# The output projection's low-weight products behind a flag read on the chip, and reordered seams, in a three-part decoder layer

## The chip, the cores and the metric

The kernel runs on one core of one Trainium2 chip. The metric is the device time of one execution in microseconds (us). Five engines work at once and wait for each other through semaphores: TensorE (PE, with its weight loads shown apart as PEld), VectorE (DVE), ScalarE (ACT), GpSimd (POOL) and SyncE (SP), which here issues all DMAs. Products are written to PSUM, in eight banks of 128 x 512 float32; the kernel uses four under the name `ps` and four under the name `pa`. POOL doesn't read PSUM here.

## The reference

One layer on 8 sequences of 112 tokens, 512 wide, in three parts, each added to x:

```
x = x + self_attention(layernorm(x))            # 16 heads of 32, rotary, causal, plain float32
x = x + cross_block(layernorm(x), ctx_2048)     # below
x = x + ffn(layernorm(x))                       # ternary weights, silu(gate) * up, rms norm

# cross_block
ln_out = LN(h)
q, k, v, qx = fp8_linear(ln_out, wq/wk/wv/wqx)              # inputs rounded to fp8
core = attention of q (16 heads of 128) on k, v (8 heads)   # over the 112 own tokens
kx, vx = split(ctx @ w_kv_x)                                # 375 context tokens, float32
xout = attention of qx on kx, vx
catq = fp8_round(concat(core, xout) / proj_smooth)
return (catq @ wproj.T) * (proj_in_scale * proj_w_scale)    # 4096 -> 512
```

The weight `wproj` is made by `_fp8_roundtrip(w / sc)`: a float32 array whose values are fp8 numbers. `w_kv_x` is a plain float32 array.

## The kernel before, in words

**Numbers.** Where a product must be as exact as float32, the kernel splits a float32 operand into a high part `hi` (rounded to float32r, the format of PE's faster products) and a low part `lo = w - hi`, and issues two products into one bank. `split_chunk(s, what, k)` (L288) does that for one 128 x 512 chunk of weights of strip `s`: `what` 0 is q, 1 is k and v, 2 is the output projection. For `what` 2 it copies on ACT and subtracts on POOL (L300, L301), then frees the raw tile, which starts the next raw load on SP (`load_raw`, L268).

**Work units.** The cross block is 8 strips of heads, 4 of the own attention and 4 of the context attention, by 8 batches: 64 units, `Own` (0 to 31) and `Context` (32 to 63). A unit's `project` is its spine on PE; between its pieces it calls `advance(stage, g)`, which runs a named stage (`normed`, `turn`, `score`, `weigh`, `turn_p`, `attend`, `rounded`, `out`) of earlier units, each with a lag in units written in `stages`. So the order on each engine is written out by hand; there is no scheduler. Rows of 7 token tiles of 128 don't match 8 batches of 112, so a unit with b of 1 to 7 also finishes tile b - 1: `rounded` (L752) rounds that tile to `cq` on ACT, DVE and POOL, and `project_out` (L704) multiplies `cq` with the strip's weights: for each of four 128-row pieces a `hi` and a `lo` product through `both` (L688, products at L691), eight into one bank, and then DVE adds the scaled bank to `xs` (L713). In the last strip DVE also takes the tile's norm statistics there (`stats3`).

**The stages in time.** Self-attention (L373 to L679) runs in plain float32: `project_qk` makes q and k for four batches at a time (PE, ACT's bias L433, DVE's shuffle, POOL's two rotary passes L444 and L446), then `batch` interleaves values, scores, softmax (DVE, POOL, ACT's exp L511), turns of p (ACT's copies L524) and their products. `transposed` (L408) turns the normed input by PE and ACT's copies L418. Then come the own units, then the context units, in whose keys the products of L912 stand, twelve for each of three pieces. During the context units the feed-forward weights are made ternary (L1119 to L1164).

**The drain and the feed-forward part.** Behind the last unit, a loop over n from 1 to 3 runs the open stages in the order of one tuple, and a table `between` puts pieces of the feed-forward part after some of them: `ffn_input(0)` (norm, L161, turns by PE, L1227, ACT's copy L1229 and DVE's subtraction L1230 for tiles 0 to 3) after the last scores, and four `hidden_part`s (sixteen products each at L1256, ACT's silu L1264) after later stages. Then `ffn_input(1)` takes tiles 4 to 6. The feed-forward part runs eight hidden steps and four `down` steps (L1389). In the last `down`, the root mean square is found (one-column products at L1405, L1409, POOL's power L133), and DVE finishes each tile with two passes (L1414, L1415), after which SP stores it (L1416).

Of the kernel before, what the change touches and what calls it, by code (L numbers as in the profile page):

```python
# [11 lines left out]
F32 = mybir.dt.float32  # L12
F32R = mybir.dt.float32r
BF = mybir.dt.bfloat16
U16 = mybir.dt.uint16
AF = mybir.ActivationFunctionType
ALU = mybir.AluOpType
AX = mybir.AxisListType

P = 128  # L20
# [3 lines left out]
KC = H // P  # L24
NT = B * S // P
# [14 lines left out]
def decoder_layer(  # L40
# [10 lines left out]
    wdown: bass.AP,  # L51
    out: bass.AP,
):

# [5 lines left out]
    nc = tc.nc  # L62
# [12 lines left out]
    def uid(s):  # L75
        count[0] += 1
        return f"{s}_{count[0]}"

    def ps():
        return psum.tile([P, 512], F32, tag="ps", name=uid("ps"))  # L80
# [5 lines left out]
    def sm(what, n, bufs=None):  # L86
        return small.tile([P, n], F32, tag=f"{what}{n}", name=uid(what), bufs=bufs)
# [7 lines left out]
    xb, xs = [], []  # L95
# [19 lines left out]
    nc.gpsimd.memset(gones, 0.0)  # L115
    nc.gpsimd.memset(gones[0:64, 0:64], 1.0 / 128.0)
    nc.gpsimd.memset(gones[64:128, 64:128], 1.0 / 128.0)


    idle = ps()  # L120
# [9 lines left out]
    def power(dst):  # L130

        rows, n = dst.shape
        nc.gpsimd.tensor_tensor(dst, dst, expo[:rows, :n], ALU.pow)  # L133
# [80 lines left out]
    raws, split = {}, {}  # L214
# [73 lines left out]
    def split_chunk(s, what, k):  # L288

        w = raws.pop((s, what, k))  # L290
        if what == 1 and s > 3:
            hi, mix, lo = [ring.tile("CBA", "wx") for _ in range(3)]
            nc.scalar.copy(hi, w)  # L293
            nc.gpsimd.tensor_tensor(w, w, hi.bitcast(F32), ALU.subtract)
            split[s, what, k] = hi, mix, lo
            opened.append((w, hi, mix, lo))
            return
        hi, lo = [ring.tile(("ABC", "B", "AB")[what], i) for i in ("hi", "lo")]
        if what == 2:
            nc.scalar.copy(hi, w)  # L300
            nc.gpsimd.tensor_tensor(lo, w, hi.bitcast(F32), ALU.subtract)  # L301
        else:
            if what == 0:
                cuts = [(slice(0, 512), 0 if s < 4 else 3)]
            else:
                cuts = [(slice(0, 256), 1), (slice(256, 512), 2)]
            for cut, m in cuts:
                c = col(V_INS + 4 * m + k)
                nc.scalar.activation(hi[:, cut], w[:, cut], AF.Copy, scale=c)
                nc.vector.scalar_tensor_tensor(  # L310
                    lo[:, cut], w[:, cut], c, hi[:, cut].bitcast(F32), ALU.mult, ALU.subtract
                )
        split[s, what, k] = hi, lo
        load_raw()
# [58 lines left out]
    with ExitStack() as st:  # L373
# [22 lines left out]
        w_v = load_qkv(wqkv[2], a1, 4)  # L396
        vb = a1.tile([S, H], F32, tag="vb", name="vb")
        nc.sync.dma_start(out=vb, in_=vbias.partition_broadcast(S))

        hT = a1.tile([P, KC, B * S], F32, tag="hT", name="hT")  # L400
        lns, hs = {}, {}
# [193 lines left out]

        for i, oc in enumerate((0, 4, 1, 5, 2, 6, 3, 7)):
            project_qk(0, oc)
            if i == 1:
                for b in range(HB, B):
                    lns[b] = norm_stats(xb[b])  # L600
            elif i == 2:
                for b in range(HB, B):
                    ln_apply(b)
            elif i == 3:
                transposed(1)
# [17 lines left out]
        def batch(b, last, begin=0):  # L623


            least = last - HB
            if b < last:
                va[b] = values(b)
            if b - 2 >= least:
                attended(b - 2, va.pop(b - 2), pt.pop(b - 2))  # L630
            if b < last:
                banks = scores(b)
            if least <= b - 1 < last:
                pt[b - 1] = turned(pr.pop(b - 1))
            for _ in range(begin):
                quantise_begin()
            if b < last:
                pr[b] = softmaxed(banks, b >= HB)

        for b in range(HB):  # L640
            batch(b, HB)
        for i, oc in enumerate((0, 4, 1, 5, 2, 6, 3, 7)):
            project_qk(1, oc)
            if i < 2:
                batch(HB + i, HB)
            if i < HB + 2:
                joined(i, 0, HB)
            if i == HB + 2:
                for _ in range(4):
                    quantise_begin()  # L650
            elif i == HB + 3:
                quantise(4, False)
# [32 lines left out]
    for k in range(KC):  # L685
        split_chunk(0, 1, k)

    def both(out_, lhsT, parts, cut, first, last):  # L688

        for i, part in enumerate(parts):  # L690
            nc.tensor.matmul(  # L691
                out_, lhsT=lhsT, rhs=part[:, cut], start=first and i == 0, stop=last and i == 1
            )
# [10 lines left out]
    def project_out(u):  # L704

        if u.b == 0:
            return
        t, po = u.b - 1, ps()
        for j in range(4):
            both(po, u.cq[:, j * P : (j + 1) * P], split[u.s, 2, j], slice(0, 512), j == 0, j == 3)  # L710
        if u.b == NT:
            drop(u.s, 2)
        nc.vector.scalar_tensor_tensor(xs[t], po, psc, xs[t], ALU.mult, ALU.add)  # L713
        if u.s == 7:
            stats3[t] = norm_stats(xs[t])
# [497 lines left out]
                nc.gpsimd.tensor_scalar_mul(d[k], ts[k // 2][:, k % 2, :], 2.0)  # L1213
        wfs[what, i] = d

    def ffn_input(half):
        cols = CUTS[half]
        n, hs = cols.stop - cols.start, []
        for i in range(n // P):
            t = cols.start // P + i  # L1220
            h = f0.tile([P, H], F32, tag="sg", name=uid("h"), bufs=4)
            norm_apply(h, xs[t], *stats3[t])
            hs.append(h)
        for k in range(KC):
            tp = ps()
            for i, h in enumerate(hs):
                nc.tensor.transpose(tp[:, i * P : (i + 1) * P], h[:, k * P : (k + 1) * P], ident)  # L1227
            hi, lo = [ring.tile("AB", "h3T", n) for _ in range(2)]
            nc.scalar.copy(hi, tp[:, :n])  # L1229
            nc.vector.tensor_tensor(lo, tp[:, :n], hi.bitcast(F32), ALU.subtract)  # L1230
            hT[half, k] = hi, lo
# [124 lines left out]
    def hidden(u, pool):  # L1356
# [3 lines left out]

    hidden(0, f0)

    between = {
        (1, "score"): lambda: ffn_input(0),
        (2, "out"): lambda: hidden_part(0, 0, 0),
        (2, "turn_p"): lambda: hidden_part(0, 1, 0),
        (2, "rounded"): lambda: hidden_part(1, 0, 0),
        (3, "out"): lambda: hidden_part(1, 1, 0),
    }
    for n in range(1, 4):  # L1370
        live = [v for v in live if v.at < len(v.stages)]
        for stage in ("normed", "weigh", "out", "turn_p", "attend", "turn", "rounded", "score"):
            advance(stage, len(units) - 1 + n)
            if (n, stage) in between:
                between[n, stage]()

    attention.close()
    f1 = ctx.enter_context(tc.tile_pool(name="f1", bufs=1))
    tpool.append(ctx.enter_context(tc.tile_pool(name="tern2", bufs=1)))
    ffn_input(1)  # L1380
    expand_w("down", 0)
    ys = [f1.tile([P, H], F32, tag=f"y{t}", name=f"y{t}") for t in range(NT)]
    def down(c, hid, last):
        wd, pos = wfs.pop(("down", c)), []
        for t in range(NT):
            po = ps()
            for k in range(4):
                for part_ in range(2):
                    nc.tensor.matmul(  # L1389
                        po,  # L1390
                        lhsT=hid[part_][:, k, t * P : (t + 1) * P],
                        rhs=wd[k],
                        start=(k == 0 and part_ == 0),
                        stop=(k == 3 and part_ == 1),
                    )
            if c == 0:
                nc.vector.tensor_copy(ys[t], po)
            elif not last:
                nc.vector.tensor_tensor(ys[t], ys[t], po, ALU.add)
            else:  # L1400
                pos.append(po)
            if last and t == 1:
                pr = ps()
                for i in range(NT):
                    nc.tensor.matmul(  # L1405
                        pr[:, i : i + 1], lhsT=sq[:, i * P : (i + 1) * P], rhs=ones1, start=True, stop=True
                    )
                rstd = sm("rms", NT)
                nc.vector.tensor_scalar(rstd, pr[:, 0:NT], 1.0 / FF, RMS_EPS, ALU.mult, ALU.add)  # L1409
                power(rstd)  # L1410
            while last and t > 0 and pos:
                i = t + 1 - len(pos)
                r = rstd[:, i : i + 1]
                nc.vector.scalar_tensor_tensor(ys[i], ys[i], r, xs[i], ALU.mult, ALU.add)  # L1414
                nc.vector.scalar_tensor_tensor(ys[i], pos.pop(0), r, ys[i], ALU.mult, ALU.add)  # L1415
                nc.sync.dma_start(out=out[i * P : (i + 1) * P, :], in_=ys[i])  # L1416

        ring.free(*wd)
# [119 lines left out]
```

## Time and profile before

| | us |
|---|---|
| median of 3 runs | 1285.17 (1284.61 to 1287.16) |
| the profiled execution | 1283.86 |
| its span, first to last instruction | 1282.1 |
| PE busy in the span | 1200.6 |
| DVE, ACT, POOL busy | 931.8, 815.8, 846.1 |
| the `lo` products of the output projection, records in all | 88.4 (224 of 395 ns) |
| POOL's subtractions L301 | 41.9 (32 of 1316 ns) |

How to read the lines that follow: a group's line gives engine, operation, out<-in by the program's names, shapes, the count after an x, and times. A timeline line gives the start and the duration in us, and in brackets how long the engine was idle just before and whose result ended that. A table by stretches gives, for each engine, the busy time and the number of instructions, then the mean granted TensorE clock, the DMA engines' share and GB/s. The slices cut the span into 40 equal parts and give the busy share of each in tenths. Records of products overlap: the rate is read from start to start.

### The profile page before, as it was taken

The page shows a single profiled execution, that of the slowest core. Times are in us where ns is not written, and L with a number is a line of the kernel's source. Part 1 is how long each engine was busy: PE and PEld are TensorE (multiplying, and loading weights), DVE is VectorE, ACT ScalarE, POOL GpSimd, SP SyncE. Part 2 cuts the span into 40 slices and gives each one's busy share as a digit, 9 for nine tenths or more (in the row PEclk, how much of TensorE's full clock was granted, in tenths as well). Part 3 has the DMA queues.
Part 4 walks back from the last instruction along what each step waited for, and adds up shares of the span by engine and source line. Part 5 has one row for each costly group of instructions (what it writes and reads, how often), then busy time and mean ns, then how long its engine had stood idle before and what let it go on. Part 6 is the DMA issues. An engine that isn't in the chain of part 4 may idle for free. (4 is left out here: it accounts for less than half of the span.)

```text
span 1282.1 us, 19634 instructions
## 1 busy us (share of the span) xinstructions
PE 1200.6 (94%) x6326; PEld 962.4 (75%) x6326; DVE 931.8 (73%) x2366; ACT 815.8 (64%) x2008; POOL 846.1 (66%) x938
## 2 busy tenths in 40 slices
PE   8997976889999889999999999999999998899998
PEld 5673765777888767888788778788777786687876
DVE  6647986887888866677776776677777775579864
ACT  2334676878687757667667767777667665456432
POOL 6657866687877756765767656667566655477762
PEclk9988886999999999999999999999999999999999
DMA  5001120213332354455554455554544440133201
GB/s 172 1 1 42 34 91 17 83 50 106 131 127 93 122 209 152 147 201 194 182 174 151 151 171 174 162 170 161 174 150 148 167 157 5 34 107 104 73 29 58
DMA packets 55511, 149.85 MB, mean 117 GB/s; under 512 B 6400, under 2 KB 15744, under 8 KB 55408
## 3 DMA queue, kind: packets, MB, share of 16 engines
q1 hardware_dynamic: 55408, 148.59, 35.3%
q8 instruction: 50, 0.82, 0.3%
q14 instruction: 53, 0.43, 0.1%
HBM read 120.18 MB, written 26.56 MB: 114 GB/s over the span
## 5 line engine op out<-in xcount | busy, mean ns | idle before, releaser
L912 PE MATMUL pa<-wx,ct 128*125 128x512 f32 x1152 | 289.4, 400 | 2.4 <-ACT wx L293 1.5
L912 PEld LDWEIGHTS pa<-wx,ct 128*125 128x125 f32 x1152 | 208.9, 186 | 51.2 <-ACT wx L293 1.9
L210 POOL TENSOR_TENSOR f8t<-y,big 128x512 f32<-128x512 bf16 (+1 forms) x88 | 107.4, 1224 | 140.2 <-DVE big L208 139.8
L738 POOL TENSOR_TENSOR p<-p,ri 112x448 f32<-112x448 f32 (+1 forms) x64 | 118.1, 1846 | 35.6 <-DVE ri L736 35.4
L923 DVE TENSOR_TENSOR kv<-kv,pa 125x512 f32<-125x512 f32 x96 | 65.9, 687 | 98.7 <-PE pa L912 52.2
L691 PE MATMUL pa<-hi,xq 128*128 128x512 f32 (+2 forms) x352 | 112.9, 345 | 11.0 <-DVE xq L368 9.2
L997 ACT ACTIVATE p<-ps,cmx 112x375 f32<-112x375 f32 x128 | 71.8, 574 | 75.5 <-DVE cmx L996 75.5
L1256 PE MATMUL pa<-h3T,wf 128*128 128x512 f32 (+1 forms) x512 | 110.0, 371 | 2.7 <-DVE sg L1266 2.7
L691 PE MATMUL pa<-lo,xq 128*128 128x512 f32 (+2 forms) x352 | 107.5, 331 | 0.9 <-DVE lo L310 0.9
L1256 PEld LDWEIGHTS pa<-h3T,wf 128*128 128x128 f32 x512 | 92.9, 188 | 14.9 <-DVE sg L1266 3.6
L174 DVE BATCH_NORM_AGGREGATE mv<-bst 128x2 f32<-128x6 f32 (+1 forms) x472 | 86.0, 182 | 16.3
L691 PE MATMUL ps<-hi,cq 128*128 128x512 f32 x224 | 90.8, 405 | 2.8 <-POOL cq L758 1.1
L730 ACT ACTIVATE qT<-ps,hln 128x448 f32<-128x448 f32 (+6 forms) x112 | 57.4, 567 | 56.1 <-PE ps L725 55.8
L691 PE MATMUL ps<-lo,cq 128*128 128x512 f32 x224 | 88.4, 395 | 0.0
L173 DVE BATCH_NORM_STATS2 bst<-pa 128x6 f32<-128x128 f32 x280 | 76.2, 272 | 16.2 <-PE pa L691 16.2
L988 PE MATMUL ps<-kT,qT 128*112 128x375 f32 x256 | 86.0, 478 | 0.5 <-ACT kT L974 0.5
L1158 POOL TENSOR_TENSOR th<-th,tw 128x512 bf16<-128x512 bf16 x48 | 59.1, 1231 | 40.1 <-DVE th L1150 40.1
L193 ACT ACTIVATE kv<-kv,ckvnm,ckvr 125x128 f32<-125x128 f32 x192 | 77.5, 491 | 6.2 <-POOL ckvnm L189 5.5
L691 PEld LDWEIGHTS pa<-hi,xq 128*128 128x128 f32 (+1 forms) x352 | 67.9, 193 | 17.3 <-DVE xq L368 10.7
L1021 PE MATMUL ps<-pT,kv 125*128 125x224 f32 x384 | 78.0, 353 | 0.0
L1021 PEld LDWEIGHTS ps<-pT,kv 125*128 125x128 f32 x384 | 72.6, 190 | 2.0
L691 PEld LDWEIGHTS pa<-lo,xq 128*128 128x128 f32 (+1 forms) x352 | 68.0, 193 | 7.4 <-DVE lo L310 3.8
(181 smaller groups left out, 3131.1 us busy)
## 6 DMA issues: line engine op xcount, KB each, us to landing
ct<-forms SPq DMA_DIRECT2D x84, 750.0 KB, 4.4
w<-in_wattn SPq DMA_DIRECT2D x96, 256.0 KB, 3.1
forms<-form SPq DMA_DIRECT2D x12, 750.0 KB, 4.7
forms<-ct SPq DMA_DIRECT2D x12, 750.0 KB, 5.1
tr<-in_wgu SPq DMA_DIRECT2D x32, 256.0 KB, 4.5
done<-th SPq DMA_DIRECT2D x48, 128.0 KB, 4.3
wh<-done SPq DMA_DIRECT2D x24, 256.0 KB, 3.7
tr<-in_wdown SPq DMA_DIRECT2D x16, 256.0 KB, 4.4
```

Source lines behind the costliest of these rows:

```text
L173: nc.vector.bn_stats(st[: self.rows], a)
L174: nc.vector.bn_aggr(self.mv[: self.rows, self.at, :], st[: self.rows])
L193: nc.scalar.activation(dst, src, AF.Identity, bias=self.nm[:rows, i : i + 1], scale=self.r[:rows, i : i + 1])
L210: nc.gpsimd.tensor_tensor(t, y16, big, ALU.add)
L691: nc.tensor.matmul(out_, lhsT=lhsT, rhs=part[:, cut], start=first and i == 0, stop=last and i == 1)
L738: nc.gpsimd.tensor_tensor(u.p, u.p, bc, ALU.mult)
L912: nc.tensor.matmul(banks[bank][:CJ, :], lhsT=ct[:, at : at + CJ] if ct.dtype == F32R else ct[:, at : at + CJ].bitcast(F32R), rhs=split[sel ...
L923: nc.vector.tensor_tensor(kv, kv, banks[1][:CJ, :], ALU.add)
L988: nc.tensor.matmul(pp[:S, :SC], lhsT=qT[:, j, :], rhs=self.kT[:, j // 2, :], start=True, stop=True,)
L997: nc.scalar.activation(self.p[:, j, :], pp[:S, :SC], AF.Exp, bias=nm[:S], accum_out=self.sums[:S, j : j + 1])
L1021: nc.tensor.matmul(po[:, cut], lhsT=self.kv[j][:, 256 + g * P : 256 + (g + 1) * P], rhs=self.pT[:, j, cut], start=(j == 0), stop=(j == NJ ...
L1256: nc.tensor.matmul(pp[:, :n], lhsT=wcur[k][:, m * 256 + blk * P : m * 256 + (blk + 1) * P], rhs=hT[half, k][i], start=(k == 0 and i == 0), ...
```

## The change

Early on, while self-attention runs, SP loads all eight strips' output-projection weights whole (1.05 MB each, two buffers), and ACT reads the low 16 bits of every float32 as integers and sums them (`look`). DVE and one PE product add the sums up, and DVE writes 1 to `flag` if the sum is above zero, else 0. PE and POOL each read the flag into a register ahead of the first unit. From then on POOL makes the low weights, and PE issues the four low products of a projection, only if the register is above 0. If it is 0, PE issues four one-column products of zeros in their place, and POOL's semaphore is stepped without work. The conditions cut the program into blocks: all five engines jump at each of the 88.

The other edits are at the seams. `ffn_input` becomes three functions, and the table `between` a written-out order: the norms and turns of tiles 0 to 3 go ahead of the turns of p of the last unit but one, and their split ahead of the last scores; two `hidden_part`s stand right behind the last scores; tiles 4 and 5 are turned ahead of the last projection, tile 6 behind the last of those `hidden_part`s. Turns are written into `pa` banks for tiles 0 to 3, and into two `ps` and two `pa` banks for the rest. In the last `down`, ACT and POOL make the first of the two passes for tiles 3 to 6.

```diff
+    flag = const.tile([1, 1], mybir.dt.int32, tag="flag", name="flag")
+    zero = const.tile([P, 1], BF, tag="zero", name="zero")
+    nc.gpsimd.memset(zero, 0.0)
...
             nc.scalar.copy(hi, w)
-            nc.gpsimd.tensor_tensor(lo, w, hi.bitcast(F32), ALU.subtract)
+            with tc.If(low_split > 0):
+                nc.gpsimd.tensor_tensor(lo, w, hi.bitcast(F32), ALU.subtract)
...
+        seen = a1.tile([P, 16], F32, tag="seen", name="seen")
+        looked = []
+        def look_load():
+            i = len(looked)
+            if i < 8:
+                w = a0.tile([P, KC * 512], F32, tag="wp", name=uid("wp"))
+                nc.sync.dma_start(out=w.rearrange("p (k o) -> p k o", k=KC), in_=wattn[i, 2])
+                looked.append(w)
+        def look(i):
+            w = looked[i].bitcast(U16).rearrange("p (n two) -> p n two", two=2)
+            for h in range(2):
+                low = w[:, h * 1024 : (h + 1) * 1024, 0:1].rearrange("p n o -> p (n o)")
+                nc.scalar.activation(low, low, AF.Copy, accum_out=seen[:, 2 * i + h : 2 * i + h + 1])
+            look_load()
+        for _ in range(2):
+            look_load()
...
             project_qk(0, oc)
+            if i in (3, 5, 7):
+                look(i // 2 - 1)
...
             batch(b, HB)
+            look(3 + b)
...
             project_qk(1, oc)
+            if i == 0:
+                look(7)
+            elif i == 2:
+                total = sm("seen", 1)
+                nc.vector.tensor_reduce(total, seen, AX.X, ALU.add)
+                pc = ps()
+                nc.tensor.matmul(pc[:1, 0:1], lhsT=total, rhs=ones1, start=True, stop=True)
+                nc.vector.tensor_scalar(flag, pc[:1, 0:1], 0.0, None, ALU.is_gt)
...
+    low = nc.values_load(flag[0:1, 0:1], engines=[mybir.EngineType.PE], min_val=0, max_val=1)
+    low_split = nc.values_load(flag[0:1, 0:1], engines=[mybir.EngineType.Pool], min_val=0, max_val=1)
...
-        for j in range(4):
-            both(po, u.cq[:, j * P : (j + 1) * P], split[u.s, 2, j], slice(0, 512), j == 0, j == 3)
+        def product(j, i, **kw):
+            nc.tensor.matmul(po, lhsT=u.cq[:, j * P : (j + 1) * P], rhs=split[u.s, 2, j][i], **kw)
+        product(0, 0, start=True, stop=False)
+        with tc.If(low > 0) as branch:
+            for j in range(4):
+                product(j, 1, start=False, stop=False)
+        with branch.Else():
+            for j in range(4):
+                nc.tensor.matmul(po[:1, 0:1], lhsT=zero, rhs=zero, start=False, stop=False)
+        for j in range(1, 4):
+            product(j, 0, start=False, stop=j == 3)
...
+    live = [v for v in live if v.at < len(v.stages)]
+    input_norms(0, 1)
+    last(1, "normed", "weigh")
+    input_norms(2, 3)
+    last(1, "out")
+    input_turns(0, 0, 1, 2, 3)
+    last(1, "turn_p", "attend", "turn", "rounded")
+    input_splits(0)
+    last(1, "score")
+    hidden_part(0, 0, 0)
+    last(2, "weigh")
+    hidden_part(0, 1, 0)
+    last(2, "turn_p", "out", "attend")
+    input_norms(4, 5)
+    last(2, "rounded")
+    hidden_part(1, 0, 0)
+    input_turns(1, 4, 5)
+    last(3, "out")
+    input_norms(6)
+    hidden_part(1, 1, 0)
...
-    ffn_input(1)
+    input_turns(1, 6)
+    input_splits(1)
...
                 power(rstd)
+                for i in range(3, NT):
+                    nc.scalar.activation(ys[i], ys[i], AF.Copy, scale=rstd[:, i : i + 1])
+                    nc.gpsimd.tensor_tensor(ys[i], ys[i], xs[i], ALU.add)
             while last and t > 0 and pos:
...
-                nc.vector.scalar_tensor_tensor(ys[i], ys[i], r, xs[i], ALU.mult, ALU.add)
+                if i < 3:
+                    nc.vector.scalar_tensor_tensor(ys[i], ys[i], r, xs[i], ALU.mult, ALU.add)
                 nc.vector.scalar_tensor_tensor(ys[i], pos.pop(0), r, ys[i], ALU.mult, ALU.add)
```

More of the change, by code (lines that the diff above doesn't have):

```diff
@@ L1214, in expand_w, with input_norms, input_turns, input_splits @@
         wfs[what, i] = d
[L1216 to L1220, printed above, removed]
+    inputs = {}
+    def input_norms(*ts):
+        for t in ts:
             h = f0.tile([P, H], F32, tag="sg", name=uid("h"), bufs=4)
             norm_apply(h, xs[t], *stats3[t])
[L1223 to L1227, printed above, removed]
+            inputs[t] = h
+    def input_turns(half, *ts):
+        first = CUTS[half].start // P
+        if ts[0] == first:
+            inputs["banks", half] = [f() for f in ((ps, ps, pa, pa) if half else (pa,) * KC)]
+        for t in ts:
+            h = inputs.pop(t)
+            for k, tp in enumerate(inputs["banks", half]):
+                nc.tensor.transpose(
+                    tp[:, (t - first) * P : (t - first + 1) * P], h[:, k * P : (k + 1) * P], ident
+                )
+    def input_splits(half):
+        n = CUTS[half].stop - CUTS[half].start
+        for k, tp in enumerate(inputs.pop(("banks", half))):
             hi, lo = [ring.tile("AB", "h3T", n) for _ in range(2)]
@@ L1361, in decoder_layer, with last @@
     hidden(0, f0)
[L1363 to L1372, printed above, removed]
-            advance(stage, len(units) - 1 + n)
-            if (n, stage) in between:
-                between[n, stage]()
+    def last(n, *stages):
+        for stage in stages:
+            advance(stage, len(units) - 1 + n)
+    live = [v for v in live if v.at < len(v.stages)]
[18 more added lines that the diff above has]
+    hidden_part(1, 1, 0)
+    assert not any(v.at < len(v.stages) for v in live)
     attention.close()
```

## The prediction

> **What bounds the kernel now.** I read the page's busy shares and slices first, then the busy times cut at the borders of the stages (seen in the timeline: self-attention to 164 us, the ramp to 233, own units to 459, context units to 1078, the drain to 1122, the feed-forward part, the tail from 1264).
>
> ```profile
> span 1282.1 us, 19634 instructions
> PE 1200.6 (94%) x6326; PEld 962.4 (75%) x6326; DVE 931.8 (73%) x2366; ACT 815.8 (64%) x2008; POOL 846.1 (66%) x938
> ...
> PE   8997976889999889999999999999999998899998
> ...
> PEclk9988886999999999999999999999999999999999
> ```
> ```profile
> core 0: us, PE busy (x) PEld busy (x) DVE busy (x) ACT busy (x) POOL busy (x), PEclk, DMA share, GB/s
> ...
> 233.00:459.00 226.00, 205.84 (x1309) 177.72 (x1307) 188.14 (x544) 174.91 (x538) 173.35 (x215) 0.99 0.32 110
> 459.00:1078.00 619.00, 607.33 (x2934) 485.24 (x2934) 438.81 (x1211) 429.46 (x1029) 397.18 (x443) 1.00 0.49 161
> 1078.00:1122.00 44.00, 35.88 (x176) 28.19 (x177) 21.87 (x43) 20.43 (x47) 18.63 (x18) 1.00 0.08 25
> ```
> TensorE sets the time. In the context stage it is busy 607.3 of 619 us (98%) and the next engine, DVE, 71%: what leaves PE there leaves the span. In the own stage PE has 91%, but DVE 83%, ACT and POOL 77%: a cut of PE is paid out in part. In the drain PE has 82%: its waits can be had by another order.
>
> How much a low product costs is read from the starts, since records overlap (mean 395 ns). All four lines are of one output projection in the timeline:
> ```profile
> 714.88 0.39 PE L691 MATMUL ps<-hi,cq 128*128 128x512 f32 x1
> ...
> 715.10 0.39 PE L691 MATMUL ps<-lo,cq 128*128 128x512 f32 x1
> ...
> 715.33 0.39 PE L691 MATMUL ps<-hi,cq 128*128 128x512 f32 x1
> ...
> 715.56 0.39 PE L691 MATMUL ps<-lo,cq 128*128 128x512 f32 x1
> ```
> Start to start 0.227 us.
>
> **1. The low products.** 56 projections (8 strips, 7 tiles) issue four each: 224 x 0.2265 = 50.7 us off PE, if the flag is 0. It should be: the weights are values rounded to fp8, three bits of mantissa, so the low 16 bits of each float32 are zero and the flag's sum is zero.
>
> In their place stand four pairs of a one-column weight load and a 1x1 product, which the trace doesn't show. From above, the products with one column and 128 float32 weight columns:
> ```profile
> 1265.22 1.62 PE L1405 MATMUL ps<-ones,sq 128*128 128x1 f32 x14
> ...
> 1266.70 9.58 PE L1389 MATMUL ps<-wf,hid 128*128 128x512 f32 x40
> ```
> 14 passes in 1.48 us from first start to next line's, 0.106 (0.112 between inner starts). From below: nothing. A bfloat16 load records 0.10 us (gones, L1141) where float32 records 0.19, so I take half, 0.056. Behind them the next high product's weight load has no long product to hide under: after the L1405 run the first product took 0.318 us to the next one instead of 0.227, 0.09 more. So 4 x 0.056 + 0.09 = 0.31 us are added per projection (ends 0.09 and 0.54), 0.906 - 0.31 = 0.59 net (0.37 to 0.82). The Trainium skill (TensorE: Matmul & The Clock Gate, "Wait — 56ns, not 53.3ns?") has a floor of about 25 ns between products however small. By that the addition would be 0.19, an estimate from that page, and the net 0.72; no run here shows it.
>
> Context: 28 x 0.59 = 16.6, at 95% **15.8 us**. Own: 16.6, at 60% **10.0 us**: with 16.6 less, PE's 205.8 falls to 189, level with DVE's 188, so about half to two thirds; ends 30% and 90%.
>
> **2. GpSimd's 32 subtractions** go: 41.9 us of POOL, about half in the own stage. POOL isn't the end of the chain there, and ACT's copy still holds the raw tile. In their place POOL waits for its own earlier instruction and adds to the semaphore (17 to 43 ns are the sequencer events' rows). I give no gain (ends 0 and -3).
>
> **3. Branches.** 56 compares on PE and 32 on POOL; every engine takes a jump at each of the 88. The trace has none; the nearest row is a sequencer's wait:
> ```profile
> L691 PEldq EVENT_SEMAPHORE  x55: 51/51/51, 162.3 to 1107.4; - x55
> ```
> PE's sequencer runs ahead of the array: the event of L988 at 568.7 stands before a load that starts at 571.2, so 2.5 us, with twelve products between. 56 compares, 56 jumps out of the short block and 32 at POOL's conditions, 144 x 0.051 = 7.3 us, lie under that cover in the context stage. In the own stage PE often waits for kT, p or xs, the cover is thin, and I count **3 us** (0 to 10). On ACT, DVE and SP 88 x 0.05 = 4.5 us are spread over a third idle.
>
> **4. Looking at the weights.** Eight 1.05 MB loads and sixteen ACT passes of 128x1024 go into the first 90 us. SP's third load waits for ACT's first look (two buffers); behind it stand the other looks' loads and the five w loads at 118 us, not due before. The first two loads queue behind 5.5 MB which took 24 us at 229 GB/s: the first lands at 24 + 1.05/0.229 = 28.6 us. ACT reaches look 0 after its fourth qb, at 23.3, and waits there. Behind it:
> ```profile
> 26.74 1.84 ACT L418 COPY hT<-ps 128x448 f32<-128x448 f32 x4 [3.47 <-PE ps L412]
> 30.11 0.63 ACT L433 ACTIVATE qb<-pa,vec 128x448 f32<-128x448 f32 x1 [1.53 <-PE pa L425]
> 33.12 0.64 ACT L433 ACTIVATE qb<-pa,vec 128x448 f32<-128x448 f32 x1 [2.37 <-POOL qb L444]
> ```
> A 512-wide pass takes 0.63 us, so a look some 2.1 to 2.9. hT then ends near 33 and the fifth qb starts 3 us late. POOL turns q and k at 3.0 us each without a break from there to the first scores at 42.4, so the 3 us reach PE. Look 1 leaves up to 0.5 over; the later ones stand in ACT's idle of 2 to 6 us between exp and copy. **3.5 us** (0 to 7). PE and POOL each read the flag into a register once, which has no row; a 128 KB DMA from issue to landing takes 4.3 us, the longest it could need, and PE waits for xq there anyway (9.2 us in two waits): **1 us** (0 to 4).
>
> **5. Seams.** In the drain:
> ```profile
> 1082.77 1.56 PE L1009 MATMUL ps<-ident,p 112*125 112x112 f32 x12 [2.54 <-POOL p L738]
> ...
> 1091.79 2.96 PE L1227 MATMUL ps<-ident,h 128*128 128x128 f32 x16 [1.14 <-ACT p L997]
> ...
> 1120.03 0.30 PE L1227 MATMUL ps<-ident,h 128*128 128x128 f32 x1 [1.64 <-DVE h L161]
> ```
> PE idles 9 us there in all. After, the 16 turns stand ahead of the p turns, in the 2.54 us; two hidden blocks follow the last scores and cover the last softmax; tiles 4 and 5 are turned ahead of the last projection, which waited 1.1 us. Laid out with these durations, the wait of 2.54, the 1.14 with what follows of the stretched turns (2.96 for 1.76), and some 2 us around 1112 to 1122 go, and about 2 us come back before the last projection, whose cq takes 4.6 us from attend. **6 us** (2 to 8). An added wait: the first norm now stands before DVE's reciprocal and waits for the last store and loads of the region it reuses; the store is issued at 1073.0 and takes 4.3 us, 1077.3 against 1078.6. If it came later, ri, p and the turns would follow one for one.
>
> Tail: DVE ends at 1279.22, after seven tiles of two passes from 1268.67 (0.75 each), while PE's last product ends at 1276.3. After, ten passes: three tiles by 1273.2, then one pass a tile behind PE; ACT (0.63) and POOL (1.3) have tiles 3 to 6 ready by 1274.5. The end is the last product plus one pass, about 1276.8: **2.4 us** (1.5 to 2.7).
>
> **Sum**: 15.8 + 10.0 + 6 + 2.4 - 3 - 3.5 - 1 = 26.7 us. The profiled execution took 1283.86 us (span 1282.1 and 1.8 around it), 1.3 under the median of the runs, so 1257.2 by it and **1258 us** by the median.
>
> **Rivals.**
> A. PE's cut is paid out whole: pairs near the low end, looks hidden: 56 x 0.75 + 8.4 - 2 = 48 less, 1237. For it: PE 98% busy. Against: DVE in the own stage. 9%.
> B. Own units become DVE's and branches show: 15.8 + 3 + 6 + 2.4 - 10 - 7 - 1 = 9, 1276. For it: DVE 83%, thin cover. 12%.
> C. **Slower**: each jump over the skipped products makes PE's sequencer fetch its code anew.
> ```profile
> q8 instruction: 50, 0.82, 0.3%
> ```
> That is 16 KB a packet, one in some 26 us, 0.3% of 16 x 1282 / 50 = 1.2 us each; 256 KB loads need 3.1 us from issue to landing. At 1.2 us past the cover, 56 x 1.2 = 67 us against 29.7: 1322 us; it decides from 0.53 us a jump. For it: no row here shows a taken jump at all. Against it: the code is read in order, and the target lies ten instructions on, in the same or the next packet's 256. The Trainium skill (Runtime: NRT & Kernel Launch, "Instruction fetch mechanics") says that a taken branch stalls where its target lies outside the present window of two pages. By that rule, estimated, some two of the 56 jumps cross a page, and nearly none leaves the window. 11%.
> D. The flag is 1 and nothing is skipped: 8.4 - 7.5 gained, 1284. 2%.
>
> My forecast, 1242 to 1272, has 66%. The range 1236 to 1280 takes in A and B at their likely ends and leaves out C and the far end of A. Faster by over 0.2% (2.6 us, about what a measurement of this kernel can tell from no change): forecast, A and nearly all of B, 86%; within: 3%, D and B's end; slower: C, 11%.
>
> **What would show it.** No L691 lo,cq line and 56 x 4 one-column products: part 1; their starts give the 0.056. High products spaced by more than a microsecond around them, or many more instruction packets: C. hT's copies at 31 us instead of 26.7: part 4. The own stage's length tells 60% from 30 or 90. DVE's last pass within 1 us of PE's last product: the tail. It is wrong if jumps stall PE, or if own units don't shorten.

## The result and the profile after

The changed kernel takes 1271.15 us in the median of four runs (1269.3 to 1275.55), the kernel before 1285.01: a ratio of 0.989, 95% interval 0.9866 to 0.9913. Six later runs gave 1275.19 against 1286.77, 0.9913 (0.9889 to 0.9937). So it is faster by about 1%, 11 to 14 us, where the prediction had 27. The first median lies inside the forecast's 1242 to 1272 by less than 1 us, the later one only inside the wider range of 1236 to 1280; the forecast's gain is about twice what came. The profiled execution is the slowest of its four (1275.55 us, span 1273.7), 8.3 us under that of before. Stages are compared in the profiled executions, verdicts rest on all runs.

The page of the changed kernel, then busy times by stretch (columns as in the prediction) from the first output projection to the first product with `wx`, and from 38 us later to the last one:

```profile
span 1273.7 us, 19767 instructions
PE 1184.0 (93%) x6328; PEld 934.7 (73%) x6328; DVE 914.6 (72%) x2364; ACT 837.8 (66%) x2044; POOL 811.0 (64%) x911
...
PEclk9978877999999989999999999999999999999999
```
```profile
246.06:463.83 217.77, 197.12 (x1322) 167.22 (x1321) 174.94 (x546) 177.06 (x547) 159.35 (x204) 0.98 0.34 117
...
502.10:1070.12 568.02, 557.98 (x2772) 439.19 (x2772) 406.73 (x1134) 406.81 (x970) 355.50 (x400) 1.00 0.50 165
```
PE has 16.6 us less of busy time and POOL 35 us less. But in the clock row sevens have come early on, and an eight at about 460 us, where before had a nine. Between six points that every version has (first product with xq, first output projection, first and last product with `wx`, first `down` product, end of the last), the stages of the profiled executions last, in us:

| | to xq | to first out | own | context | drain | down | end | halved windows |
|---|---|---|---|---|---|---|---|---|
| before | 164.2 | 68.7 | 228.8 | 613.0 | 64.0 | 137.6 | 5.8 | 18 |
| after | 178.1 | 68.0 | 217.8 | 606.3 | 61.6 | 138.0 | 4.0 | 28 |
| seams only | 166.0 | 67.6 | 227.2 | 615.1 | 61.2 | 138.3 | 4.1 | 20 |
| flag constant | 167.8 | 67.7 | 217.7 | 604.7 | 60.1 | 137.7 | 4.2 | 23 |
| no branch | 161.9 | 68.9 | 216.0 | 597.0 | 59.3 | 139.0 | 4.1 | 19 |
| all mended | 163.9 | 68.9 | 214.2 | 605.0 | 59.5 | 139.0 | 3.8 | 21 |

A halved window is 3.41 us in which the granted clock is 0.5 (last section). 24 projections lie in the own column, 29 in the context column, 3 in the drain's.

**What is lost first.** The first cross-attention product comes 13.9 us late. TensorE's waits there, after and then before (line, releaser, us, times, longest):

```profile
PE ps L553 <- ACT pt L557: 3.5, 2, 2.9
...
PE ps L686 <- DVE seen L684: 2.6, 1, 2.6
...
PE ps L485 <- ACT pt L557: 2.4, 1, 2.4
PE ps L553 <- DVE o L580: 1.3, 1, 1.3
```
```profile
PE ps L520 <- ACT pt L524: 0.4, 1, 0.4
```
And ACT's timeline, after:
```profile
49.91 0.58 ACT L544 ACTIVATE p<-p 112x448 f32<-112x448 f32 x1 [0.61 <-POOL p L541]
50.40 1.34 ACT L427 ACTIVATE wp<-wp 128x1024 uint16<-128x1024 uint16 x1
...
52.96 1.81 ACT L557 COPY pt<-ps 112x448 f32<-112x448 f32 x4
```
The look (two passes of 1.34 us and two reads of the sum) stands between the last exp and the copies of the turned p. Before, these copies began at 50.23. Over this stage all of TensorE's waits add up to 15.3 us, 7.4 before, and it runs more often at half clock, which loses 20.8 us up to this point against 13.8: 7.9 + 7.0 is the 13.9 us to within one.

**What the skipped block leaves.** The same projection's place in the timeline, in the changed kernel:
```profile
505.87 0.40 PE L758 MATMUL ps<-hi,cq 128*128 128x512 f32 x1
506.19 0.24 PE L767 MATMUL ps<-zero 128*1 128x1 bf16 x4
506.36 0.97 PE L758 MATMUL ps<-hi,cq 128*128 128x512 f32 x3
```
The flag is 0, here and in every run that has one, so the other side of the branch was never timed. Start to start, one projection reads 327, 26, 25, 25, 94, 335, 235, 232 ns, 1.30 us, where the eight products took 1.84 (own: 1.38 for 1.93). The one-column products themselves stand 25 ns apart, the floor that the Trainium skill gives (TensorE: Matmul & The Clock Gate, "Wait — 56ns, not 53.3ns?"): on that point the trace agrees. But the first comes 0.1 us late, and the next high products lose 0.2.

### The profile page after: what moved, and what is told of

The parts are those of the page before. It is cut to its first block, busy times and chain, and to the rows that moved or that the text cites. A ratio compares the mean times of both kernels' runs of the same rounds, so it can differ in the third digit from the quotient of the medians.

```text
span 1273.7 us, 19767 instructions
## 1 busy us (share of the span) xinstructions
PE 1184.0 (93%) x6328; PEld 934.7 (73%) x6328; DVE 914.6 (72%) x2364; ACT 837.8 (66%) x2044; POOL 811.0 (64%) x911
## 5 line engine op out<-in xcount | busy, mean ns | idle before, releaser
L184 DVE BATCH_NORM_STATS2 bst<-pa 128x6 f32<-128x128 f32 x280 | 76.0, 272 | 20.9 <-PE pa L738 20.8
L1217 POOL TENSOR_TENSOR th<-th,tw 128x512 bf16<-128x512 bf16 x48 | 59.5, 1240 | 38.2 <-DVE th L1209 38.2
L758 PE MATMUL ps<-hi,cq 128*128 128x512 f32 x224 | 81.3, 445 | 2.3 <-DVE x L772 1.5
L738 PEld LDWEIGHTS pa<-hi,xq 128*128 128x128 f32 (+1 forms) x352 | 69.4, 197 | 17.5 <-DVE xq L380 10.7
L817 POOL TENSOR_TENSOR cq<-f8t,big 128x512 fp32r<-128x512 f32 x56 | 65.1, 1163 | 4.4
```

What stands on the lines that cost most here:

```text
L184: nc.vector.bn_stats(st[: self.rows], a)
L738: nc.tensor.matmul(out_, lhsT=lhsT, rhs=part[:, cut], start=first and i == 0, stop=last and i == 1)
L758: nc.tensor.matmul(po, lhsT=u.cq[:, j * P : (j + 1) * P], rhs=split[u.s, 2, j][i], **kw)
```

## The experiments

All twelve, with ratios to the kernel before on the same chip:

| | median, us | ratio | 95% |
|---|---|---|---|
| seams only | 1280.97 | 0.9967 | 0.9954 to 0.9979 |
| flag constant, no looks | 1264.07 | 0.9843 | 0.9827 to 0.9858 |
| zeros, no branch | 1264.08 | 0.9822 | 0.9799 to 0.9844 |
| no branch at all | 1251.26 | 0.9737 | 0.9723 to 0.975 |
| no branch, subtractions kept | 1262.41 | 0.9815 | 0.9788 to 0.9842 |
| the changed kernel again | 1275.19 | 0.9913 | 0.9889 to 0.9937 |
| one product of zeros | 1270.86 | 0.9884 | 0.9865 to 0.9903 |
| zeros in fp32r | 1268.16 | 0.9857 | 0.9832 to 0.9881 |
| looks late | 1271.83 | 0.9889 | 0.9869 to 0.991 |
| looks late, product later | 1263.0 | 0.9821 | 0.9793 to 0.9849 |
| all mended | 1253.32 | 0.9738 | 0.9711 to 0.9764 |
| all mended, weighing split | 1251.64 | 0.9719 | 0.9689 to 0.975 |

**The seams alone.**
```diff
-        with tc.If(low > 0) as branch: ...
+        for j in range(4):
+            both(po, u.cq[:, j * P : (j + 1) * P], split[u.s, 2, j], slice(0, 512), j == 0, j == 3)
```


> Only the seams of the change: all low products and subtractions unconditionally as before, no flag, looks or branches. Theory 1 (read from the changed kernel's trace: its drain from the last context-key product to the first down product is 2.4 us shorter, of which 1.6 us are its three shorter projections, and its end behind TensorE's last product is 1.8 us shorter): 0.8 + 1.8 = 2.6 us, 1282.4 us. Rival (the seams are worth the 8.4 us of the prediction when the projections keep their length, since there the rearranged order has longer products to hide under): 1276.6 us.

Measured 4.2 us (2.7 to 5.9): between the two, nearer to the theory. The drain is 2.8 us shorter and the end behind TensorE's last product 1.7. In the changed kernel's drain two waits have come in the place of the old ones:
```profile
1078.63 1.12 PE L1291 MATMUL pa<-ident,h 128*128 128x128 f32 x4 [2.17 <-DVE h L172]
...
1097.68 1.63 PE L1068 MATMUL ps<-ident,p 112*125 112x112 f32 x12 [1.92 <-POOL p L797]
```
Twelve of the sixteen turns run where TensorE had waited 2.54 us for p; the last four then wait for the fourth tile's norm on VectorE. And the last softmax is covered by two hidden blocks only until 1095.8: TensorE stands 1.92 us for POOL's p. All its waits in the drain sum to 5.8 us, 7.9 before.

**The looks' price.**
```diff
+    nc.gpsimd.memset(flag, 0)
-        for _ in range(2):
-            look_load()
```
(and without the looks, the sum, its product and the compare)

> The flag is set to zero by one GpSimd memset; the eight wp loads, the sixteen ScalarE looks, the sum, its 1x1 product and the compare are left out (so the weights are not looked at). Branches, one-column products and seams stay as in the changed kernel. Theory 1 (the looks cost the early 13.9 us: the looks after the softmax blocks stand on ScalarE ahead of the pt copies for which TensorE waits, and TensorE's clock is halved in more stretches there): the first cross-attention product comes at about 165 us instead of 178.1, and the time is 1271.2 - 13 = 1258 us (1254 to 1262). Rival (the early loss is the flag's read, the memsets or the clock by itself, and the looks cost the 3.5 us of the prediction): the first product at 174 us or later, 1267 to 1271 us.

Measured 0.9843 where the changed kernel had 0.989 and 0.9913: the looks cost 0.5 to 0.7%, 6 to 9 us. The first xq product comes at 167.8. Theory 1 holds for the place; the size is between the two. Part of the profile's 13.9 us is scatter: the profiles without looks have that point anywhere from 161.9 to 167.8, with 5 to 9 halved windows ahead of it.

> The changed kernel again, word for word, on the chip of the runs beside it, to give the differences a firmer base than its four runs did. Expected from those: 1269 to 1273 us. Theory (the looks after the softmax blocks cost the early time): its first cross-attention product at 174 to 178 us and TensorE waiting for the pt copies; if its median comes out at 1271, the looks are worth 7 us by the constant flag's 1264.1, if at 1274, 10 us.

176.6 us to the first xq product and 2.4 and 2.9 us of waits for the copies: the same picture again, at 1275.19 us, above the 1269 to 1273 expected.

**Is it place or amount?** The looks at other places:
```diff
             batch(b, HB)
-            look(3 + b)
+            if b in (1, 2):
+                look(2 + b)
...
             project_qk(1, oc)
-            if i == 0:
-                look(7)
+            if i in (2, 3, 5):
+                look({2: 5, 3: 6, 5: 7}[i])
...
             quantise(4, False)
+            if b == HB + 2:
+                total = sm("seen", 1)
+                ...
```


> The same eight loads and sixteen looks as in the changed kernel, at other places: looks 0 to 2 as before, 3 and 4 after the softmax blocks 1 and 2 (behind which ScalarE was idle 4 to 5 us before the pt copies), 5 to 7 behind the q and k projections 2, 3 and 5 of the second half; the sum, its product and the compare three softmax blocks later. Theory 1 (the place is what costs: looks ahead of pt copies, and a product that waits for the sum): most of the looks' price goes, 1264 to 1267 us, first cross-attention product at 165 to 168 us. Rival (the amount is what costs, 24 us more of ScalarE and 8 MB more of loads wherever they stand): as the changed kernel, 1270 to 1272 us.

Measured 0.9889, as the changed kernel in its first runs, 3 us under it in its later ones on the same chip: by the time alone the rival wins. The trace says otherwise. The long waits for the copies are gone (0.6 us in all), and one other stands there:
```profile
148.97 0.19 PE L700 MATMUL ps<-ones,seen 128*1 128x1 f32 x2 [7.58 <-DVE seen L698]
```
I had put the sum's product right behind the sum, which VectorE reaches only after a softmax block's work; TensorE, which issues in order, stood for it. So the next run moves the product alone:
```diff
                 nc.vector.tensor_reduce(total, seen, AX.X, ALU.add)
+            elif b == B - 1:
                 pc = ps()
```


> The looks at the later places, and the 1x1 product with the sum's compare one softmax block behind the sum instead of right behind it: in the run with the late looks TensorE stood 7.6 us before that product, since the sum stands on VectorE behind a softmax block. Theory (each look and the sum cost only where TensorE waits for them in order, and 24 us of ScalarE passes and 8 MB of loads are free elsewhere): that wait goes whole, first cross-attention product at 165 to 168 us, 1271.8 - 7 = 1265 us (1261 to 1268), level with the constant flag. Rival (the amount of the looks is what costs): another wait takes its place, 1269 us or more.

```profile
155.91 0.19 PE L701 MATMUL ps<-ones,seen 128*1 128x1 f32 x2
```
No wait there, 1263.0 us, 0.9821: level with the kernel that doesn't look at all (0.9843), and 0.9% below the changed kernel (0.9913; two chips, each ratio to the kernel before on its own). 24 us of ScalarE and 8 MB of loads cost nothing measurable at the right places. The theory holds.

**Branch or zeros?** Without `If`, once with the zeros and once without:
```diff
-        with tc.If(low > 0) as branch: ...
+        for j in range(4):
+            nc.tensor.matmul(po[:1, 0:1], lhsT=zero, rhs=zero, start=False, stop=False)
```


> As the run without a branch, but with the four one-column products of zeros unconditionally behind the first high product (they add zero). It tells the branch's own cost from that of the one-column products. Theory 1 (the branch is hidden under the sequencer's lead; the 0.38 us are the one-column weight loads, 97 ns ahead of the first, 3 x 25 between them and 0.1 twice behind): the same spacing as in the changed kernel, 327, 26, 25, 25, 94, 335 ns, and the time within 2 us of the constant flag. Rival (the 97 ns ahead of the first are the jump): the first spacing falls to about 230 ns, and the time is 56 x 0.1 x 80% = 4.5 us or more below the constant flag.

Spacing 327, 26, 25, 26, 93, 334: the same to the nanosecond or two. Theory 1: the jump isn't in it, and the time doesn't tell 88 branches from none (1264.08 against 1264.07; the ratios, 0.2% apart, overlap).

> As the run with the constant flag, and without any branch: the flag's two register reads, the conditions, the low products, the one-column products and GpSimd's subtractions are all left out (so the low half of these weights is never used). Each output projection is then four high products, about 4 x 0.229 = 0.92 us instead of 1.30 (context) and 1.38 (own). Theory 1 (what stands in the block's place costs 0.38 to 0.46 us of TensorE each, paid out like the products): 28 x 0.38 x 90% + 28 x 0.46 x 60% = 17 us below the constant flag, 1241 us. Rival (the context units are by now bound elsewhere: the turn of p waits for GpSimd's weighing, whose waits grew from 4.7 to 7.5 us): half of it, about 1250 us, with the waits of the p turns for POOL at 10 us or more in the context stage.

1251.26 us, 12.8 under the constant flag: nearer to the rival. A projection takes 0.93 us here (own 1.02), so the block's rest was 0.37 and 0.36 us, not the 0.46 that I had for the own units; 12.8 is 62% of 56 x 0.37 = 20.7 us of TensorE. The waits of the p turns in the context stage, in before, after and this kernel:
```profile
PE ps L1009 <- POOL p L738: 4.7, 9, 0.8
```
```profile
PE ps L1068 <- POOL p L797: 7.5, 9, 1.4
```
```profile
PE ps L1044 <- POOL p L773: 10.3, 10, 1.7
```
The same nine places wait in all three (a tenth, of 0.2 us, comes in the last). At six of them the wait grows by what a projection loses: before it is 0.3 to 0.8 us, in the changed kernel 0.5 us more, in this one 0.9 to 1.1 us more, so there the cut is worth nothing. The three others, 0.3 to 0.6 us, don't grow. The chain from scores over exp and POOL's pass to p hasn't become shorter. From the seams alone to this kernel, the context stage falls 18.1 us where its 29 projections lose 29 x 0.92 = 26.7; these waits and those for pT (0.7 to 2.4) take back 7.3 of the 8.6 missing.

**POOL's subtractions alone.**
```diff
             nc.scalar.copy(hi, w)
+            nc.gpsimd.tensor_tensor(lo, w, hi.bitcast(F32), ALU.subtract)
```


> As the run without a branch (no flag, looks, branches, low or one-column products), but with GpSimd's 32 subtractions that make the unused low weights kept. Theory (they are worth nothing, since TensorE waits for GpSimd little in the own stage): within 2 us of the run without a branch, 0.974 of the kernel before. Rival (42 us of GpSimd, 21 of them in the own stage, hold up its weighing of p): 4 us or more above it, with longer waits of the p turns for POOL.

0.9815 against 0.9737: the subtractions, which I had put at nothing, are worth 0.8%, 10 us, once the products are gone. The rival wins. The own stage is 7.4 us longer, and TensorE waits there 4.1 us more for VectorE's addition to x, 1.9 more for POOL's p (kept, then gone):
```profile
PE ps L900 <- POOL p L774: 8.9, 11, 2.8
...
PE ps L864 <- DVE x L749: 5.8, 6, 1.9
```
```profile
PE ps L899 <- POOL p L773: 7.0, 9, 2.2
...
PE ps L863 <- DVE x L748: 1.7, 5, 0.7
```
Why VectorE comes late can be read where the same strip and batch stand in both traces (DVE's and POOL's rows; L219 is VectorE's bfloat16 pass over y ahead of the rounding; kept, then gone):
```profile
343.61 0.93 POOL L774 TENSOR_TENSOR p<-p,ri 112x448 f32<-112x448 f32 x1
344.01 3.15 DVE L219 TENSOR_SCALAR y<-y 128x512 bf16<-128x512 bf16 x1 [0.55 <-ACT big L215]
344.50 1.29 POOL L313 TENSOR_TENSOR lo<-w,hi 128x512 fp32r<-128x512 f32 x1
345.75 1.27 POOL L1095 TENSOR_TENSOR form<-raw,form 128x500 fp32r<-128x500 f32 x1
```
```profile
338.82 0.93 POOL L773 TENSOR_TENSOR p<-p,ri 112x448 f32<-112x448 f32 x1
339.22 1.90 DVE L219 TENSOR_SCALAR y<-y 128x512 bf16<-128x512 bf16 x1 [0.54 <-ACT big L215]
339.71 1.26 POOL L1094 TENSOR_TENSOR form<-raw,form 128x500 fp32r<-128x500 f32 x1
```
With nothing on POOL beside it, this pass takes 0.28 to 0.30 us (38 of its 56 places). Here it ends only when POOL's row of passes has ended, and the subtraction makes that row longer: 3.15 us against 1.90. Three such places in the own stage are followed by TensorE's waits of 1.4, 1.5 and 1.9 us for the addition to x. The profiles also differ in the context stage (601.8 against 597.0), but there this one has three more halved windows, which cost 5.1 us; whether the subtractions bring those, the run doesn't tell.

**What makes the zeros dear: number or kind?**
```diff
-            for j in range(4):
+            for j in range(1):
                 nc.tensor.matmul(po[:1, 0:1], lhsT=zero, rhs=zero, start=False, stop=False)
```


> One one-column product in the place of the skipped block instead of four. Theory 1 (of the 0.38 us, 3 x 0.025 are the products themselves, the rest the two changes of weights around them): spacing 327, 94, 335 ns, 56 x 0.076 = 4.2 us less of TensorE, 55% of it paid out: 2 to 3 us below the changed kernel. Rival (the weights of one column cost by their number): 56 x 0.28 = 16 us less, 8 us or more paid out.

Spacing 327, 94, 337: as theory 1 has it, 75 ns less a projection. 0.9884 against 0.9913: 3.7 us, the intervals overlap.

```diff
-    zero = const.tile([P, 1], BF, tag="zero", name="zero")
+    zero = const.tile([P, 2], F32R, tag="zero", name="zero")
...
-                nc.tensor.matmul(po[:1, 0:1], lhsT=zero, rhs=zero, start=False, stop=False)
+                nc.tensor.matmul(po[:2, 0:2], lhsT=zero, rhs=zero, start=False, stop=False)
```


> The four products of zeros with weights and columns in the projections' own type (fp32r, two columns instead of one) instead of bfloat16. Theory 1 (the 97 ns ahead of the first and the 0.1 behind are the price of any weight load that has no long product to hide under, whatever the type): 0.38 us as before, or more, since a float32 load records 187 ns and a bfloat16 one 79; time as the changed kernel's or some us above. Rival (it is the change of type that keeps the load from running under the product before): the first spacing falls to 230 ns, and the time by 56 x 0.1 x 55% = 3 us or more.

```profile
747.98 0.40 PE L758 MATMUL ps<-hi,cq 128*128 128x512 f32 x1
748.22 0.24 PE L767 MATMUL ps<-zero 128*2 128x2 f32 x4
748.32 0.93 PE L758 MATMUL ps<-hi,cq 128*128 128x512 f32 x3
```
235, 27, 25, 26, 26, 313, 226, 230: 1.11 us instead of 1.30, and 0.9857. The rival wins: the bfloat16 product of one column begins 0.1 us late, and the first high product behind it as well. Whether it is the type as such or the form isn't told apart, since the program holds a bfloat16 product as two instructions, load and product, and an fp32r one as one. The type alone is not enough, as other bfloat16 products between fp32r ones show, here in before:
```profile
716.46 0.39 PE L691 MATMUL ps<-lo,cq 128*128 128x512 f32 x1
716.69 0.10 PEld L1141 LDWEIGHTS <-gones 128*128 128x128 bf16 x1 [0.26 <-issue]
716.69 0.39 PE L1141 MATMUL ps<-ta,gones 128*128 128x512 bf16 x1
...
716.92 1.46 PE L1009 MATMUL ps<-ident,p 112*125 112x112 f32 x12
```
Their weight load isn't issued early either (the load path idles 0.26 us ahead of it), but with 512 columns the product starts 0.23 us behind the one before and the next 0.23 us behind it, as fp32r products do. Why the one-column product comes late stays open.

**All mended.** The product later, and one fp32r product of zeros:

> As the run with the product later, with one product of zeros in the projections' own type (two columns) in the place of the skipped block instead of four in bfloat16. By the two spacings measured apart (four fp32r 1.12 us a projection; one bfloat16 1.23; both 1.30) it should be 235 + 26 + 313 + 2 x 230 = 1.03 us, 56 x 0.27 = 15 us less of TensorE. Theory (55% paid out, as between the seams alone and the constant flag): 8 us below the run beside it, about 1257 us (1253 to 1260). Rival (the turn of p waits for GpSimd in the place of most of it): 3 us or less below it.

1.04 us a projection in the context stage (1.13 in the own), 1253.32 us, 0.9738: 9.7 us under the run beside it by the medians, 10.7 by the ratios, a little over the theory's 8. This version keeps everything the change does, beats both kernels, and is as fast as leaving branch, flag and zeros out.

```diff
-        nc.gpsimd.tensor_tensor(u.p, u.p, bc, ALU.mult)
+        if u.s > 3:
+            nc.gpsimd.tensor_tensor(u.p[:, 0:2], u.p[:, 0:2], bc[:, 0:2], ALU.mult)
+            nc.vector.tensor_tensor(u.p[:, 2:4], u.p[:, 2:4], bc[:, 2:4], ALU.mult)
```


> As the all-mended run, and in the context units GpSimd's pass over p (p times 1/sum, 1.9 us) is halved between GpSimd and VectorE by heads. Theory (what the context units don't pay out is TensorE's wait for that pass, 7.5 us after against 4.7 before and 10.3 where the whole block is gone): these waits fall below 3 us and the time by 4 to 7 us. Rival (VectorE's half comes no earlier, being queued behind other VectorE work, or delays it): the waits move to VectorE's half, and the time stays within 2 us or gets longer.

The p turns' wait for POOL in the context stage falls from 9.4 to 5.2 us, and the stage from 605.0 to 596.8 in the profiles, 3.4 of it by two halved windows less. The medians differ by 1.7 us with overlapping intervals, which is the rival's time. So the wait is where I said, though it fell to 5.2 and not below 3; that removing it pays isn't shown.

## Why the prediction was right, and where its terms were not

The sign, the state of the flag and the range were right; the sum, 26.7, was not. That the first median still fell inside 1242 to 1272 is partly luck, since terms that failed stood on both sides. Against it, from the ratios: seams 4.2, skipped work with zeros and branches 15.9 (seams only to constant flag, 0.0124 x 1285), looks -6 to -9: 11 to 14 us.

- **Low products, context, "at 95%"**: 15.8 forecast. This is the term that failed. The stage was 98% busy with PE, and I read from that that nothing could come late behind it. Of its idle time, 11 us, 4.7 were nine waits of the p turns, each at the end of its own chain through POOL, and at six of them the wait takes the whole cut. 29 x 0.55 = 16.0 us gross gave 10.4 from seams only to constant flag, and 29 x 0.54 = 15.6 gave 6.7 from before to after. The latter's missing 8.9: 4.8 us of longer waits, 4.5 of them for p and pT, 3.4 us from two halved windows where before had none, 0.7 unexplained.
- **Own, "at 60%"**: 10.0 forecast, 9.5 and 11.0 measured. The size was right, by luck as far as the runs tell. 24 projections lie there and not 28, so the gross is 24 x 0.55 = 13.2. DVE doesn't become level with PE: it falls to 175 us itself, under PE's 197. And part of the gain may be the subtractions', which the sum had at nothing: with all 24 x 0.92 = 22.0 us of products gone but the subtractions kept, the stage is only 3.8 us shorter than with the seams alone (227.2 to 223.4, 3.4 us of the missing being two more halved windows); the other 7.4 come when the subtractions go too. How the 9.5 to 11.0 divide wasn't run.
- **The zeros**: 0.31 us forecast, 0.37 measured, inside its ends of 0.09 and 0.54, but made up otherwise: 25 ns each and not 56, then 0.1 ahead of the first, which I didn't have, and 0.17 behind the last instead of 0.09.
- **POOL's subtractions**, "no gain (ends 0 and -3)": wrong, 10 us with the products gone, outside both ends. I judged POOL by its share, 77%, and not by what queues behind its passes, on VectorE too. With the zeros in place they weren't run apart.
- **Branches**, -3: not shown. Without them it is 2.7 us less by the ratios, give or take 3.5, and the spacing around the block is the same. A condition on TensorE's sequencer takes 0.20 us, four times the row that the sum used, but it runs ahead: the one at 730.99 belongs to a projection whose first weight load is at 734.67, and all 56 end before the first product of zeros starts, the closest 0.12 us before. Nor is there anything of rival C: the instruction queue moved 52 packets (50 before).
- **Looks**, -3.5: mechanism right (ACT's order passes it to PE), place wrong, and about twice as dear. Look 0 didn't wait until 28.6 us: its tile was there at 24.9, and the first scores came 0.17 us late. The looks in "ACT's idle of 2 to 6 us between exp and copy" cost, because that idle isn't there behind the first and the last of these softmax blocks; and I gave the sum's product no price, on a TensorE that issues in order.
- **Seams**, 6 and 2.4: 4.2 together. The tail's 1.7 to 1.8 us is close. In the drain the waits of 2.54, 1.14 and 1.64 us went as laid out, but the fourth norm (2.17 us) and the last p (1.92) came late in their place.
- **The flag's read**, -1: 0.5 us on each of the two engines, with no longer ramp (68.0 us against 68.7).
- **Rival B** (1276) is near the number of the later runs, but not by its mechanism: the own stage got shorter by as much as forecast and branches don't show. A fell with the waits for p. D fell with the flag.

What no term held: a wait also costs clock. Ten more halved windows than before, 28 against 18, cost 17 us of TensorE's time: four of them lie ahead of the first xq product and two each in the own, context and drain stages. It isn't the one profile alone: the mean granted clock is 0.969 to 0.978 in all runs of the kernel before and 0.959 to 0.969 in those of the changed one.

## What to carry to other kernels

A stage that is 98% busy on one engine doesn't pay a cut of that engine in full: look up what its last 2% wait for, since that chain keeps its length while the work that covers it shrinks. An engine far from full can still matter, as POOL's subtractions did: look at what stands behind its passes on other engines. Work put "into idle time" of an in-order engine costs nothing only if no other engine's next step is queued right behind it, so give each such place its own look in the timeline, and separate a result from the engine that has to fetch it. And where small filler products go between large ones, measure the spacing around them in the neighbours' type too.

## What the runs showed of the hardware

**The clock is granted in windows of 3.413 us, and half a window's idle time can be enough to lose one.** In all fourteen profiles every stretch at 0.5 that isn't cut by the end of the profile is a whole number of such windows, on a fixed grid. From 240 us on, 78 windows at half clock follow one at full clock: in 75 of them TensorE had been idle 1.54 us or more in the window before (least 1.29). Of 4007 full windows behind a full one, none followed more than 1.92 us of idle time. The Trainium skill (TensorE: Matmul & The Clock Gate, "Part 1: The HAM clock gate (the "warmup" mystery)") has the window's length and the half rate, as here, and lets the clock fall after an idle window; here about half a window did it (1.54 of 3.41 us is 45%). So two waits of 1.5 and 0.9 us about 2 us apart, as stand at 464 us in before and at 466 us after, halve the clock or not by where the grid happens to lie: the clock fell after, and not before. Each such window costs 1.7 us where TensorE is the bound.

**Products of one column** stand 25 ns apart in bfloat16, 26 in fp32r with two columns. Between fp32r products of 512 columns, a group of the bfloat16 ones starts 0.1 us late, and the products behind it lose 0.1 us more than behind the fp32r ones (1.30 us a projection against 1.11).

**A bfloat16 pass of VectorE can be held up by POOL.** The 128x512 pass over y takes 0.28 to 0.30 us with nothing on POOL beside it and up to 3.15 us beside a row of POOL passes (no branch, subtractions kept). The float32 addition to x takes 0.72 to 0.75 us in either case.
